# Moving a softmax's additions and a normalization's scaling from VectorE to GpSimd

## Chip, cores and metric

The kernel runs on one core of a Trainium2 chip. The metric is the device time of one execution in microseconds (us), as a median over runs. The engines of the core are TensorE (PE in the profile; its weight loads stand apart as PEld), VectorE (DVE), ScalarE (ACT), GpSimd (POOL) and SyncE (SP). Each has its own queue and takes its instructions in order; they wait for one another through semaphores.

## What is computed

A transformer block in float32 on x of 8 x 512 x 1024: softmax attention with 32 heads, a gated feed-forward layer, a causal sigmoid attention with 4 heads, and the same feed-forward layer again, each behind a layer norm and with its result added to x. The change touches the first part alone:

```python
def _layernorm(x, axis=-1, eps=1e-05):
    m = jnp.mean(x, axis=axis, keepdims=True)
    v = jnp.var(x, axis=axis, keepdims=True)
    return (x - m) / jnp.sqrt(v + eps)

def _L0_attn_a_ref(x, attn_qkvw, attn_qkvb, attn_ow, attn_ob):   # x is layer-normed
    HEADS = 32
    B, S, H = x.shape
    hd = H // HEADS
    scale = 1.0 / np.sqrt(hd)
    qkv = x @ attn_qkvw + attn_qkvb
    ...
    scores = jnp.einsum('bhqd,bhkd->bhqk', q, k) * scale
    probs = jax.nn.softmax(scores, axis=-1)
    ctx = jnp.einsum('bhqk,bhkd->bhqd', probs, v)
    ctx = jnp.transpose(ctx, (0, 2, 1, 3)).reshape(B, S, H)
    return ctx @ attn_ow + attn_ob

x = x + _L0_attn_a_ref(_layernorm(x, axis=-1), ...)
x = x + _L0_ffn_ref(_layernorm(x, axis=-1), ...)
x = x + _L0_attn_b_ref(_layernorm(x, axis=-1), ...)
x = x + _L0_ffn_ref(_layernorm(x, axis=-1), ...)
```

## The kernel before

The attention is cut into 64 units. Unit n is batch n // 8 and a group g = n % 8 of four heads, which together fill the 128 partitions. The loop over n (from line 1039) writes out by hand the order in which every engine gets its instructions: there is no scheduler, and what is written first is queued first.

A unit has four steps i of 128 keys or queries each. In step i the loop asks for

- `rows_step(n + 1, i)`: scores of the next unit with 128 queries on the partitions (L905, into the PSUM tile `sc`), and on DVE the row maxima with their sign turned (L906, `nmax`), which read `sc`;
- `between()`: a share of the side tasks and of the filler. The side tasks are small steps on DVE and DMA issues, kept in the queue `side` and spread over the five calls of a unit by `places`. The filler is PE work of other units: projections of unit n + 2 (L578, seven Strassen products gathered by L156 and L158), output projections (L788), and tiles of the next stage;
- `keys_step(n, i)`: the maxima are spread over `sc` by a matmul with ones (L934), the scores with keys on the partitions are added (L937), and ACT takes the exp of 128 x 2048 elements into a tile `pT` (L939). `pT` has three buffers, `sc` has one, which `rows_step` and `keys_step` share;
- `sum_step`: the four `pT` tiles of a unit are added up, as the softmax's denominators need it, into one tile `sum`. The first addition, of tiles 0 and 1, is made by GpSimd in two halves of 128 x 1024 (L948) behind the second exp. The other two are made by DVE, each one instruction of 128 x 2048 (L950): tile 2 is added ahead of step 3's `keys_step`, tile 3 in the first step of the next unit, behind its first `rows_step`.

`values_step` multiplies the exp tiles with v (L961) in step 2 and in step 0 of the next unit. `normalize(n - 1)` then sums `sum` over the partitions with a matmul (`den`, L973) and divides. At the end of a unit `split_max(n + 1)` cuts the finished maxima of the next unit into three bfloat16 parts, with five short DVE instructions: casts of `nmax` or `rest` into `parts` (L912, L914, L916) and subtractions of what the cast kept (L913, L915). Then, in step 0 of the next unit, `turn_max` turns the parts with PE (`tpm`, printed under L578) and ACT copies them into `shift` (L926), which L934 reads.

While the groups of batch b run, `norm_tasks(b + 1)` prepares the next batch. The turned x (`xT`, loaded as such) gets its layer norm there: statistics of the rows (L241, L242), the root by GpSimd (L249), one row of factors and one of shifts sent to DRAM and spread over all partitions (L550, L554), and then `apply` on `xT`: four pairs of a multiplication and an addition of 128 x 1024 elements (L558), by DVE. Eight lists of such tasks are handed out: lists 0 and 1 in unit g = 0, 2 and 3 in g = 1, 4 in g = 2, and the last three, with `apply` in them, in g = 3, 4 and 5. In g = 6 `left_tasks` forms the sums of `xT` that the projections multiply.

GpSimd's queue also holds DMA issues: weight sums (L613, L753) in the first nine units, rows of x after the attention (L816) and turned tiles (L876) later, and the roots of the layer norms (L249).

Of the kernel before, what the change touches and what calls it, by code (L numbers as in the profile page):

```python
# [17 lines left out]
ALU = mybir.AluOpType  # L18
# [8 lines left out]
TPB = S // P  # L27
# [3 lines left out]
GH = P // HD_A  # L31
# [42 lines left out]
class Filler:  # L74
# [47 lines left out]
    def run(self, count):  # L122

        while self.queue and count:
            count -= self._run_one() > 0
# [295 lines left out]
def softmax_attention(tc, cst, stage, filler, clusters, pools, dr, late, args):  # L421
# [11 lines left out]
    nc, small, ps_m = tc.nc, stage.small, stage.ps_m  # L433
# [16 lines left out]
    units, half = B * NC, NC // 2  # L450
# [25 lines left out]

    once = [partial(ow_source, RIGHT[k], c) for k in UPPER for c in range(half)]
    ows = Stream(nc, owpool, OW_BUFS, [P, S], "ow", once * (2 * B - 1))
    used, side, tiles, waiting, ready, held = {"w": 0}, deque(), deque(), deque(), deque(), []

    def first_norm():

# [37 lines left out]
    def norm_tasks(b):  # L520

        xT, st = xTp.tile([P, NC, S], F32, tag="xT", name=f"xT_{b}"), {}
        xTs[b] = xT

        def idle():
            pass

        def load(i):  # L530
            st[i] = xpool.tile([P, H], F32, tag="x", name=f"x_{b}_{i}")
            nc.sync.dma_start(st[i], x[ts(b * TPB + i, P), :])

        def turned(k):
            nc.sync.dma_start(xT[:, ts(k, 2), :], xT_in[b, :, ts(k, 2), :])

        def stats(i):
            if i == 0:
                st["mv"] = small.tile([P, TPB, 2], F32, tag="ln_mv", name="ln_mvs")
            stage.stats(st.pop(i), st["mv"][:, i, :])  # L540

        def root():
            st["rows"] = small.tile([P, 2, TPB], F32, tag="ln_rows", name="ln_rows")
            stage.rstd(st["mv"], TPB, st["rows"][:, 0, :])

        def shift():
            stage.shifts(st["mv"], st["rows"][:, 0, :], st["rows"][:, 1, :])

        def send():
            nc.sync.dma_start(dr.rows[b].rearrange("(k t p) -> p k t", k=2, p=P), st["rows"])  # L550

        def spread():
            st["all"] = xpool.tile([P, 2, S], F32, tag="x", name=f"rows_{b}")
            nc.sync.dma_start(st["all"].rearrange("p k s -> p (k s)"), dr.rows[b].partition_broadcast(P))  # L554

        def apply(k, j):
            part, rows = xT[:, ts(j, 2), :], st["all"][:, k, :].unsqueeze(1).to_broadcast([P, 2, S])
            nc.vector.tensor_tensor(part, part, rows, (ALU.mult, ALU.add)[k])  # L558

        scaled = [partial(apply, k, j) for j in range(NC // 2) for k in range(2)]  # L560
        return [
            [partial(load, 0), partial(load, 1)],
            [partial(turned, k) for k in range(NC // 2)] + [partial(stats, 0), partial(stats, 1)],
            [partial(load, 2), partial(load, 3)],
            [idle] * 3 + [partial(stats, 2), partial(stats, 3)],
            [root, shift, send, idle, spread],
            [idle, idle, *scaled[:3]],
            [idle, idle, *scaled[3:6]],
            [idle, idle, *scaled[6:]],
        ]  # L570

    width = [P]
# [98 lines left out]
    def left_tasks(b):  # L671

        xT = xTs[b]
        a11, a12, a21, a22 = (xT[:, ts(k, half), ts(m, 2 * P)] for m in range(2) for k in range(2))
        sums = (sump.tile([P, half, 2 * P], F32, tag=f"s{k}", name=f"s{k}_{b}") for k in (1, 2, 4))
        lefts[b], steps = left_sums(nc, a11, a12, a21, a22, *sums)
        return [lambda: run(enumerate(steps[:2])), *steps[2:]]
# [240 lines left out]
    def turn_max(n):  # L918

        st = state[n]  # L920
        tp = ps_m.tile([P, TPB, P], F32, tag="mm", name="tpm")
        for qt in range(TPB):
            part = parts[n % 2][:, qt, :, :].rearrange("p h c -> p (h c)")
            product(tp[:, qt, :], part, cst.ident_h, start=True, stop=True)
        st["shift"] = shiftp.tile([P, S], BF16, tag="shift", name=f"shift_{n}")
        nc.scalar.copy(st["shift"], tp.rearrange("p t q -> p (t q)"))  # L926
# [15 lines left out]
    def sum_step(n, kt):  # L942

        st = state[n]
        if kt == 1:
            st["sum"] = tmp.tile([P, GH, S], F32, tag="sum", name="sum")
            for h in (slice(0, GH // 2), slice(GH // 2, GH)):
                nc.gpsimd.tensor_tensor(st["sum"][:, h, :], st["pT", 0][:, h, :], st["pT", 1][:, h, :], ALU.add)  # L948
        else:
            nc.vector.tensor_tensor(st["sum"], st["sum"], st["pT", kt], ALU.add)  # L950

    def values_step(n, k):

# [30 lines left out]
    places, ow_later, last_sums, carried = [0], [], [], []  # L984

    def between(sides=True, form=2 * HD_A):


        if sides:
            for _ in range(-(-len(side) // places[0])):  # L990
                side.popleft()()
            places[0] -= 1
        width[0] = form
        filler.take()

    def mix_tile(near, wait):
        norm, logits = tiles.popleft()(blocks=wait)
        filler.mix(norm[:2], 0 if near else 2, 2 if near else 5)
        filler.mix(norm[2:], 9 if near else 14, 3)
        if wait:  # L1000
            waiting.append(logits)
        elif near:
            filler.mix(logits[:1], 16, 4)
            carried.extend(logits[1:])
        else:
            filler.mix(logits, 22, 4)

    def weave(pieces, products):

        out, at = [], 0  # L1010
        for j, product in enumerate(products):
            upto = 2 * round(len(pieces) * (j + 1) / (len(products) + 1) / 2)
            out += pieces[at:upto] + product
            at = upto
        return out + pieces[at:]
# [23 lines left out]
    for n in range(units):  # L1039
        b, g = divmod(n, NC)  # L1040
        ahead = n + 2
        if n == NC - 2:
            weights.fill(W_BUFS)
        if n == NC:
            run(next(outs))
            ows.fill(OW_BUFS)
        count = 0
        if n > NC:
            count = OUT_SHARES[(n - 1) % half] if n <= units - NC else LAST_SHARES[n - units]
        products = [next(outs) for _ in range(count)]  # L1050
        if ahead < units:
            if g == NC - 2:
                side.extendleft(reversed(left_tasks(b + 1)))
            filler.add(weave(project_pieces(ahead), products), mark=ahead)
        else:
            filler.add(weave([], products))
        ready.extend(waiting)
        waiting.clear()
        if tiles:
            mix_tile(n == units - 1, ahead < units)  # L1060
        side.extend(ow_later)
        ow_later.clear()
        if n == NC - 1:
            side.extend(last_sums)
        for c in OUT_SUMS.get(n, ()):
            load, steps = ow_sum_tasks(c)
            side.append(load)
            (ow_later if c == 0 else side).extend(steps)
        if b + 1 < B:
            if g == 0:  # L1070
                norms = deque(norm_tasks(b + 1))
            if g < 2:
                run(enumerate(norms.popleft()))
            if norms:
                side.extend(norms.popleft())
        side.extend(held)
        held.clear()
        filler.plan(FILLER_SHARES)
        places[0] = TPB + 1
        for i in range(TPB):  # L1080
            if n + 1 < units:
                rows_step(n + 1, i)
            if i == 0 and n > 0:
                sum_step(n - 1, TPB - 1)
            between()
            if i == 0:
                turn_max(n)
                between()
            if i == TPB - 1:
                sum_step(n, i - 1)  # L1090
            keys_step(n, i)
            if i == 1:
                sum_step(n, i)
            if i == 0 and n > 0:
                values_step(n - 1, 1)
                if ready:
                    by_cluster, by_token = ready.popleft()
                    run([by_cluster])
                    filler.mix([by_token], 6, 1)
                normalize(n - 1)  # L1100
            if i == 2:
                values_step(n, 0)
            between(False, HD_A if i in (0, 2) and n > 0 else 2 * HD_A)
        if n + 1 < units:
            split_max(n + 1)
        if ahead < units:
            filler.until(ahead)
    width[0] = P
    sum_step(units - 1, TPB - 1)
    ready = [make() for make in tiles]  # L1110
    tiles.clear()
    run(ready[0][0][:1])
# [8 lines left out]
    for i, (start, end) in enumerate(((0, 4), (4, 8), (8, 10), (10, 14))):  # L1121
        if i:
            ready = [make() for make in tiles]
# [601 lines left out]
```

## Time and profile before

| | |
|---|---|
| time, median of 3 runs | 3715.23 us (3713.79 to 3715.59) |
| span of the profiled execution | 3715.1 us |
| mean granted TensorE clock | 0.999 |
| PE busy, 356 to 2244 us (units 8 to 55) | 1886.08 of 1887.73 us |
| DVE busy, same stretch | 1336.87 us |
| ACT busy, same stretch | 502.98 us |
| GpSimd busy, same stretch | 264.00 us |

The profiled execution's span and the median of the runs are 0.1 us apart, so times of single rows can be set against the time of a run. The stretch of units 8 to 55 is periodic: a batch of eight units takes some 315 us. In it the sum of DVE's work is 71% of the time, GpSimd's 14%. A group of instructions in the profile is told by its line, engine, operation and tiles, as "L950 DVE TENSOR_TENSOR sum<-sum,pT"; behind the count stand busy time, the mean of one in ns, and the engine's idle time ahead of it, with what ended it.

### The profile page before, as it was taken

How to read it: one execution, taken by the hardware profiler on the slowest of the kernel's cores; microseconds unless marked ns; L12 is line 12 of the kernel's file. 1: busy time of each engine (PE TensorE's matmuls, PEld its weight loads, DVE VectorE, ACT ScalarE, POOL GpSimd, SP SyncE). 2: the span in 40 equal slices, each digit the busy share in tenths (PEclk: the TensorE clock that was granted, in tenths of full speed). 3: DMA queues.
4: the chain of work that ended last, by engine and by line, in shares of the span. 5: the costliest groups of instructions: out<-in, count | busy, mean ns of one | idle time of the engine just before them, and what ended most of it. 6: DMA issues, size and time to landing. Idle time of an engine off the chain costs nothing.

```text
span 3715.1 us, 76365 instructions
## 1 busy us (share of the span) xinstructions
PE 3677.4 (99%) x32792; PEld 1876.7 (51%) x32792; DVE 2539.7 (68%) x3497; ACT 927.8 (25%) x1017; POOL 594.9 (16%) x574
## 2 busy tenths in 40 slices
PE   8999999999999999999999999999999999999999
PEld 4444544544545455445445445444444467774444
DVE  4777676767667677766767767666788845556656
ACT  1222222222222222222222222222111144430000
POOL 1222111111111111111111111111000044530000
PEclk9999999999999999999999999999999999999999
DMA  5335444645655555465465454347566767763332
GB/s 184 113 122 179 142 143 147 192 138 157 185 153 150 159 162 163 133 198 152 139 182 159 143 150 124 122 156 244 158 180 179 184 186 234 222 220 127 133 132 98
DMA packets 728641, 598.55 MB, mean 161 GB/s; under 512 B 322152, under 2 KB 574064, under 8 KB 728304
## 3 DMA queue, kind: packets, MB, share of 16 engines
q1 hardware_dynamic: 701072, 496.40, 46.6%
q0 software_dynamic: 22912, 81.54, 5.7%
q10 hardware_dynamic: 4320, 15.73, 1.0%
q8 instruction: 259, 4.24, 0.5%
q14 instruction: 78, 0.64, 0.0%
HBM read 459.30 MB, written 134.25 MB: 160 GB/s over the span
## 4 chain that ended last, share of the span: by engine, by line
PE 95%; DVE 3%; DMA 1%; issue 1%; ACT 0%; POOL 0%; SPq 0%; DVEq 0%; ACTq 0%; POOLq 0%
PE mm L578 42%; PE dense L1285 20%; PE sc L905 7%; PE av L961 6%; PE sc L937 6%; PE csc L1347 4%; PE o L1366 4%; PE sc L934 2%; PE logitsT L339 1%; PE den L973 1%; PE tp L291 1%; DVE nmax L906 1%; DVE sum L950 1%; PE tpm L578 0%; DVE s L1377 0%
## 5 line engine op out<-in xcount | busy, mean ns | idle before, releaser
L906 DVE TENSOR_REDUCE nmax<-sc 128x4 f32<-128x2048 f32 x256 | 586.0, 2289 | 295.3 <-PE sc L905 295.2
L939 ACT ACTIVATE pT<-sc 128x2048 f32<-128x2048 f32 x256 | 480.8, 1878 | 1122.3 <-PE sc L937 1122.3
L948 POOL TENSOR_TENSOR sum<-pT,pT 128x1024 f32<-128x1024 f32 x128 | 309.4, 2438 | 750.0 <-ACT pT L939 678.1
L578 PE MATMUL mm<-xT,w 128*64 128x256 f32 (+1 forms) x3736 | 428.1, 383 | 0.0
L578 PEld LDWEIGHTS mm<-xT,w 128*64 128x64 f32 (+1 forms) x3736 | 241.5, 135 | 204.1 <-issue 54.3
L578 PE MATMUL mm<-s,w 128*32 128x256 f32 (+1 forms) x3672 | 321.2, 381 | 1.2 <-DVE qk L158 1.2
L950 DVE TENSOR_TENSOR sum<-sum,pT 128x2048 f32<-128x2048 f32 x128 | 292.0, 2281 | 0.9 <-ACT pT L939 0.9
L905 PE MATMUL sc<-qk,qk 32*64 32x512 f32 x4096 | 285.1, 613 | 0.5 <-ACT pT L939 0.4
L156 DVE TENSOR_TENSOR u<-dense,u 128x512 f32<-128x512 f32 x223 | 148.0, 685 | 184.7 <-PE dense L1285 169.3
L578 PEld LDWEIGHTS mm<-s,w 128*32 128x32 f32 (+1 forms) x3672 | 180.4, 122 | 180.4 <-issue 68.9
L937 PE MATMUL sc<-qk,qk 32*128 32x512 f32 x2048 | 263.7, 589 | 0.0
L578 PE MATMUL mm<-ow,ctxT 128*32 128x512 f32 (+2 forms) x1276 | 247.2, 599 | 3.0 <-DMA ow<-o_T 2.8
L961 PE MATMUL av<-pT,v 128*32 128x512 f32 x2048 | 246.4, 598 | 0.2 <-ACT pT L939 0.2
L1285 PE MATMUL dense<-sum,s 128*128 128x512 f32 x512 | 231.8, 593 | 0.0
L578 PEld LDWEIGHTS mm<-w,xT 128*64 128x64 f32 (+1 forms) x3888 | 197.5, 133 | 62.2 <-issue 48.9
L578 PE MATMUL mm<-w,xT 128*64 128x128 f32 (+1 forms) x3888 | 218.1, 274 | 0.0
L158 DVE SCALAR_TENSOR_TENSOR qk<-mm,qkvb_s,qk 128x256 f32<-128x256 f32 x224 | 107.6, 480 | 123.2 <-PE mm L578 119.2
L1285 PE MATMUL dense<-wT_s,dT_b 128*128 128x512 f32 x384 | 171.2, 593 | 0.0
L1285 PE MATMUL dense<-wT_s,dT_a 128*128 128x512 f32 x384 | 171.2, 593 | 0.0
L578 PE MATMUL mm<-ow,c 128*64 128x512 f32 (+2 forms) x864 | 169.9, 596 | 0.2 <-DMA ow<-in_ow 0.2
L578 PE MATMUL mm<-w,s 128*64 128x128 f32 x2688 | 162.5, 274 | 0.0
L578 PEld LDWEIGHTS mm<-w,s 128*64 128x64 f32 x2688 | 148.0, 137 | 22.9 <-issue 22.9
(236 smaller groups left out, 4468.8 us busy)
## 6 DMA issues: line engine op xcount, KB each, us to landing
w<-in_qkvw SPq DMA_DIRECT2D x252, 256.0 KB, 3.0
ow<-o_T SPq DMA_DIRECT2D x240, 256.0 KB, 3.6
w<-qk_T SPq DMA_DIRECT2D x224, 256.0 KB, 2.8
ow<-in_ow SPq DMA_DIRECT2D x180, 256.0 KB, 3.3
w<-v_T SPq DMA_DIRECT2D x112, 256.0 KB, 2.7
x<-in_x SPq DMA_DIRECT2D x32, 512.0 KB, 5.3
dT_a<-xT SPq DMA_DIRECT2D x32, 512.0 KB, 5.7
x_a<-x SPq DMA_DIRECT2D x32, 512.0 KB, 6.5
```

The source lines that it names most:

```text
L156: nc.vector.tensor_tensor(out, acc, other, ALU.add)
L578: nc.tensor.matmul(out[cols], lhsT[:, cols], rhs, **flags)
L905: nc.tensor.matmul(sc[ts(j, P // 2), h, :], st["q"][rows, cols], st["k"][rows, :], start=True, stop=True)
L906: nc.vector.tensor_reduce(st["nmax"][:, qt, :], sc, AX.X, ALU.max, negate=True)
L937: nc.tensor.matmul(sc[:, h, :], st["k"][rows, ts(kt, P)], st["q"][rows, :], start=False, stop=True)
L939: nc.scalar.activation(pT, sc, AF.Exp, scale=SCALE_A)
L948: nc.gpsimd.tensor_tensor(st["sum"][:, h, :], st["pT", 0][:, h, :], st["pT", 1][:, h, :], ALU.add)
L950: nc.vector.tensor_tensor(st["sum"], st["sum"], st["pT", kt], ALU.add)
L961: nc.tensor.matmul(st["av"][rows, :], st["v"][:, kt, rows], pT[:, h, :], start=(kt == 0), stop=(kt == TPB - 1))
L1285: nc.tensor.matmul(st["acc"], st["left"][LEFT[k]][:, c, :], self.w[RIGHT[k]][:, c, :], start=(c == 0), stop=(c == half - 1),)
L1347: nc.tensor.matmul(sc[:, AT_OFF[i] : AT_OFF[i] + n], k[:, c, ts(i, P)], xT[:, c, i * P :], start=(c == 0), stop=(c == 1),)
L1366: nc.tensor.matmul(acc[:, j - jj, :], at[:, start : start + P], self.v[b * TPB + i][:, cols], start=(i == 0), stop=(i == j),)
```

## The change

All three additions of a unit are made by GpSimd, each in two halves of 128 x 1024, and each is queued directly behind the `keys_step` that made its second operand: tiles 0 and 1 in step 1 as before, tile 2 in step 2, tile 3 in step 3. `apply` runs on GpSimd too. Its tasks no longer go into `side` but into a queue of their own, `slow`, which `between` empties in its second and third call of a unit, around `turn_max` and in step 1. The three lists lose the `idle` places that they began with, and `side` is shorter by them.

```diff
-    used, side, tiles, waiting, ready, held = {"w": 0}, deque(), deque(), deque(), deque(), []
+    used, side, slow, tiles, waiting, ready, held = {"w": 0}, deque(), deque(), deque(), deque(), deque(), []
...
             part, rows = xT[:, ts(j, 2), :], st["all"][:, k, :].unsqueeze(1).to_broadcast([P, 2, S])
-            nc.vector.tensor_tensor(part, part, rows, (ALU.mult, ALU.add)[k])
+            nc.gpsimd.tensor_tensor(part, part, rows, (ALU.mult, ALU.add)[k])
...
-            [idle, idle, *scaled[:3]],
-            [idle, idle, *scaled[3:6]],
-            [idle, idle, *scaled[6:]],
+            scaled[:3],
+            scaled[3:6],
+            scaled[6:],
...
             st["sum"] = tmp.tile([P, GH, S], F32, tag="sum", name="sum")
-            for h in (slice(0, GH // 2), slice(GH // 2, GH)):
-                nc.gpsimd.tensor_tensor(st["sum"][:, h, :], st["pT", 0][:, h, :], st["pT", 1][:, h, :], ALU.add)
-        else:
-            nc.vector.tensor_tensor(st["sum"], st["sum"], st["pT", kt], ALU.add)
+        before = st["pT", 0] if kt == 1 else st["sum"]
+        for h in (slice(0, GH // 2), slice(GH // 2, GH)):
+            nc.gpsimd.tensor_tensor(st["sum"][:, h, :], before[:, h, :], st["pT", kt][:, h, :], ALU.add)
...
             places[0] -= 1
+            if TPB - 2 <= places[0] < TPB and slow:
+                for _ in range(-(-len(slow) // (places[0] - TPB + 3))):
+                    slow.popleft()()
...
-                side.extend(norms.popleft())
+                (slow if len(norms) < 4 else side).extend(norms.popleft())
...
-            if i == 0 and n > 0:
-                sum_step(n - 1, TPB - 1)
             between()
             if i == 0:
                 turn_max(n)
                 between()
-            if i == TPB - 1:
-                sum_step(n, i - 1)
             keys_step(n, i)
-            if i == 1:
+            if i:
                 sum_step(n, i)
...
     width[0] = P
-    sum_step(units - 1, TPB - 1)
```

## Prediction

> **What bounds the kernel now.** I read the page's busy times first, then its chain of waits, then the groups of the lines that the diff touches.
>
> ```profile
> PE 3677.4 (99%) x32792; PEld 1876.7 (51%) x32792; DVE 2539.7 (68%) x3497; ACT 927.8 (25%) x1017; POOL 594.9 (16%) x574
> PE 95%; DVE 3%; DMA 1%; issue 1%; ACT 0%; POOL 0%; SPq 0%; DVEq 0%; ACTq 0%; POOLq 0%
> L948 POOL TENSOR_TENSOR sum<-pT,pT 128x1024 f32<-128x1024 f32 x128 | 309.4, 2438 | 750.0 <-ACT pT L939 678.1 <-ACT lg_a L350 40.3 <-DVE c L785 31.6
> L950 DVE TENSOR_TENSOR sum<-sum,pT 128x2048 f32<-128x2048 f32 x128 | 292.0, 2281 | 0.9 <-ACT pT L939 0.9
> L558 DVE TENSOR_TENSOR xT<-xT,rows 128x1024 f32<-128x1024 f32 x56 | 73.1, 1308 | 0.2
> ```
>
> TensorE (PE) is busy 99% of the span, and 95% of the chain is PE. From 356 to 2502 us, nearly all of the 64 attention units, PE's waits name VectorE (DVE) for 1.4 + 1.2 + 1.0 = 3.6 us in all. So relief for DVE is worth at most that, and the question is whether a new wait reaches PE. For that I read the timeline at the end of a unit (unit 39; columns: start and duration in us, engine, line, operation, tiles).
>
> ```profile
> 1602.42 1.88 ACT L939 ACTIVATE pT<-sc 128x2048 f32<-128x2048 f32 x1 [8.43 <-PE sc L937]
> ...
> 1605.42 0.19 DVE L912 CAST parts<-nmax 128x16 bf16<-128x16 f32 x1
> 1605.65 0.18 DVE L913 TENSOR_TENSOR rest<-nmax,parts 128x16 f32<-128x16 f32 x1
> ...
> 1605.87 0.20 DVE L914 CAST parts<-rest 128x16 bf16<-128x16 f32 x1
> ...
> 1606.11 0.19 DVE L915 TENSOR_TENSOR rest<-rest,parts 128x16 f32<-128x16 f32 x1
> 1606.33 0.20 DVE L916 CAST parts<-rest 128x16 bf16<-128x16 f32 x1
> 1606.41 2.28 DVE L906 TENSOR_REDUCE nmax<-sc 128x4 f32<-128x2048 f32 x1
> ...
> 1607.79 0.39 PE L578 MATMUL tpm<-ident_h,parts 128*64 128x128 bf16 x8
> ...
> 1609.84 0.40 PE L934 MATMUL sc<-shift,ones_h 32*128 32x512 bf16 x4
> ...
> 1612.76 1.04 PE L973 MATMUL den<-sum,ones 128*32 128x512 f32 x8
> ```
>
> Call t the end of a unit's fourth exp, here 1602.42 + 1.88 = 1604.30. The split of the next unit's maxima (L912 to L916) runs on DVE from t+1.12 to t+2.23; PE turns its result (tpm) at t+3.49, uses the scores' PSUM again (L934) at t+5.54 once nmax L906 has left it, and needs the finished sum (den) at t+8.46.
>
> Last, two places of the timeline where a GpSimd addition met DVE work; the single line at 157 us runs beside the second half of an addition pair that GpSimd ends at 158.71.
>
> ```profile
> 2361.97 0.68 DVE L785 TENSOR_TENSOR c<-ctxT 128x512 f32<-128x512 f32 x1
> ...
> 2362.65 5.25 POOL L948 TENSOR_TENSOR sum<-pT,pT 128x1024 f32<-128x1024 f32 x2 [31.59 <-DVE c L785]
> 2362.69 2.93 DVE L785 TENSOR_TENSOR c<-c,ctxT 128x512 f32<-128x512 f32 x1
> ...
> 2365.54 2.28 DVE L906 TENSOR_REDUCE nmax<-sc 128x4 f32<-128x2048 f32 x1
> ...
> 2367.87 0.40 PE L934 MATMUL sc<-shift,ones_h 32*128 32x512 bf16 x4 [0.86 <-DVE nmax L906]
> ```
>
> ```profile
> 157.87 0.87 DVE L248 TENSOR_SCALAR ln_rows<-ln_mvs 128x4 f32<-128x4 f32 x1
> ```
>
> A DVE addition of two SBUF operands, 0.69 us elsewhere, took 2.93: it was issued just after a GpSimd half-addition (2.41 us each) had begun and ended at 2365.62, 0.56 us after that one's end at 2365.06. GpSimd's second half then ended at 2367.90, 2.28 us after DVE. They take turns, an instruction at a time. L248, with one SBUF operand, took 0.87 instead of 0.16 and ended 0.03 us after the half-addition beside it. PE felt the first case: 0.86 us idle at L934. L906, which reads PSUM, is never slowed (2.28 to 2.29).
>
> **The change, part by part.**
>
> *Two DVE additions a unit go.* 128 x 2.28 = 292 us of DVE; worth 0 to 3.6 us on PE. I take 0.
>
> *Four half-additions a unit come on GpSimd*, 2.41 and 2.37 us a pair. After the fourth exp they end at t+0.15+4.78 = t+4.93, and den comes at t+7.2 to t+9.5 in units 0 to 61 and at t+6.6 in unit 62: hidden, and without that cover each would cost up to 4.9. An exp tile has three buffers, so up to unit 62 the next write of one comes over 15 us after its addition can start. In unit 63 there is no cover: its exps end at 2511.18, 2514.84 and 2520.35, so the additions run 2511.3 to 2516.1 and 2516.1 to 2520.9, two DMA issues of 0.57 follow, and the last runs 2522.1 to 2526.9; den stood at 2522.82. **+4.1.**
>
> *Where the additions lie.* The split follows gathers that wait for PE, so it stays where it is from unit 6 on, and the new pair of half-additions runs from t+0.15 to t+2.56 and on: over it. L913 and L915 read two SBUF operands. L912, L914 and L916 read one, and the trace shows no such cast beside GpSimd. Bounds: freely, as L248 of one element a partition does (11 times beside a GpSimd multiply, 0.15 us), or turn by turn, as L248 of four elements did. A cast from SBUF runs at the two-fold rate (L1434, 1024 elements, 0.674 us; L415 from PSUM, 512 elements, 0.692), so I take it to use what the additions use, and let it wait.
>
> *The price of a unit.* A released instruction ends 0.05 to 0.06 us after GpSimd's (its 0.19 or 0.20 less the 0.13 that 0.69 - 0.56 shows); GpSimd's next takes 2.28. So the locked ones leave at t+2.62, 4.95, 7.28, 9.61, 11.94, as long as GpSimd has something queued. Without a scaling behind it, GpSimd is empty after the second: L912 leaves at 2.62, L913 at 4.95, L916 at 5.65 (0.70 further, as in the rows), tpm starts at 5.71. Late by 5.71 - 3.49 = 2.22. Late next is nmax: 5.53 to 7.82, L934 at 7.87 instead of 5.54 + 2.22: 0.11 more. 2.33 in units 0, 4, 5, 7 of a batch; where tpm and L934 stood at 3.55 and 5.71 (unit 1) 2.16; at 4.36 and 6.41 (unit 6) 1.46.
>
> *The scaling* (56 operations of 1216 ns on DVE, alone; 2.3 to 2.4 on GpSimd) is put behind that pair: the order of GpSimd's queue in the changed kernel has three of them directly behind the last addition of a batch's unit 2, two behind that of unit 3, one behind that of unit 4, before anything that waits. Its rows have landed by then (issued at t-7.5, 7.8 to land). They keep the turns going: unit 2, L916 leaves at 11.94, tpm 12.00 against 4.36, and 0.11: 7.75. Unit 3: L915 at 9.61, tpm 9.89 against 3.70: 6.19. Unit 4: L914 at 7.28, tpm 7.80 against 3.49, and 0.11: 4.42.
>
> A batch: 3 x 2.33 + 2.16 + 7.75 + 6.19 + 4.42 + 1.46 = 28.97; six batches (units 8 to 55) **+173.8**. Units 6, 7 and 56 to 62, by the same t+5.71 against their tpm (t+2.62, 2.88, 2.63, 2.88, three of the first kind, one of 1.46, t+2.51): 3.09 + 2.83 + 3.08 + 2.83 + 6.99 + 1.46 + 3.20 = **+23.5**. In units 0 to 5 the split waits only for the DVE addition that goes, so it moves ahead of t: 0.
>
> *Queues.* PE's, ACT's and SP's orders are unchanged. GpSimd's DMA issues (x1, turned x, weight sums) fall up to 5 us later behind additions; what reads them comes a stage or at least a unit later: 0.
>
> Sum: 173.8 + 23.5 + 4.1 = 201.4. On the profiled execution's 3715.1 us: **3916**; the runs' median, 3715.23, is the same within 0.2 us.
>
> [...]
>
> **The rivals.**
>
> *The casts pass freely* (for it: L248 of one element; against: the two-fold rate). L913 leaves at 2.61, GpSimd's second half ends at 4.89, L915 leaves at 4.94, L916 at 5.16, tpm 5.22: 1.84 in units 0, 4, 5, 7; 1.67, 0.97, 1.52, 0.97 in 1, 2, 3, 6; the scaling costs nothing. 6 x 12.49 + 23.5 - 9 x 0.49 + 4.1 = 98.1: 3813.
>
> [...]
>
> *Not slower*: 16 elements slip past GpSimd's reads as the one-element L248 does. It decides if L913 beside a half-addition stays under 1.2 us, the room between L916 and tpm in most units. Then at most 3.6 and the 1.4 of den's wait are won and 4.1 lost: 3714 to 3719, 3717. Against it: 4 elements (L248) and 64 (L394, 1.30 instead of 0.23) waited.
>
> *More than the turns*: DVE's lateness reaches gathers or weights too, over 3960.
>
> **How the numbers follow.** Forecast 0.60, casts free 0.19, one turn 0.06, not slower 0.07, more 0.08. The forecast's own range: down to 3841 if the scalings come too late to take turns (units 2 to 4 then cost 1.46, 2.01 and 2.33: 6 x 12.56 less), up to 3927 if GpSimd's turns take 2.41. The range takes in the casts-free case: 3800 to 3960. A change under 0.2% (7.4 us) can't be told from none: faster 0.02, same 0.05, slower 0.93.
>
> **What would show it.** Right: L912 and L913 about 1.4 and 2.2 us long, PE's waits for tpm on DVE L916 near 190 us, L906 unchanged, DVE's busy time not lower by 365 us. The casts decide between forecast and first rival: L914 and L916 of 2 us in units 2 to 4 of a batch, or 0.2. Wrong if split instructions stay at 0.2 us beside GpSimd, or if PE waits at den or the exps on GpSimd.

## The result and the profile after

The changed kernel takes 3967.05 us (median of four runs, 3965.66 to 3967.57) against 3714.82 us: a ratio of 1.0677, with a 95% interval of 1.0662 to 1.0692. That is 252 us more, where the forecast was 201 and the range ended at 3960. The page of the kernel after, its busy times and its chain of waits:

```profile
PE 3750.1 (95%) x32792; PEld 1895.9 (48%) x32792; DVE 2461.9 (62%) x3313; ACT 933.9 (24%) x1017; POOL 1323.7 (33%) x886
PE 87%; DVE 10%; DMA 1%; issue 1%; POOL 0%; SPq 0%; ACT 0%; DVEq 0%; POOLq 0%; ACTq 0%
```

DVE now holds 10% of the chain, and DVE's busy time fell by 78 us only, though 365 us of instructions left it. And PE, whose instructions are the same 32,792 in the same order, is busy 72.7 us longer (3750.1 against 3677.4). The view of PE's waits (what waited, for what; us in total, times, the longest) has two lines that the change touches, first as they were before, then after:

```profile
PE tpm L578 <- DVE parts L916: 1.3, 2, 1.0
PE den L973 <- DVE sum L950: 1.4, 1, 1.4
...
PE tpm L578 <- DVE parts L916: 180.3, 58, 7.4
PE den L972 <- POOL sum L949: 3.4, 2, 2.8
```

Where DVE's time went is told by the groups of the split's lines, which took 185 to 203 ns each before, beside the maxima L906, which kept their 2.29 us, and GpSimd's new work:

```profile
L906 DVE TENSOR_REDUCE nmax<-sc 128x4 f32<-128x2048 f32 x256 | 586.0, 2289 | 318.7 <-PE sc L905 318.7
L913 DVE TENSOR_TENSOR rest<-nmax,parts 128x16 f32<-128x16 f32 x64 | 130.2, 2035 | 2.2
L912 DVE CAST parts<-nmax 128x16 bf16<-128x16 f32 x64 | 71.5, 1116 | 0.1
L914 DVE CAST parts<-rest 128x16 bf16<-128x16 f32 x64 | 52.5, 820 | 2.2
L915 DVE TENSOR_TENSOR rest<-rest,parts 128x16 f32<-128x16 f32 x64 | 37.3, 582 | 2.2
L916 DVE CAST parts<-rest 128x16 bf16<-128x16 f32 x64 | 25.4, 398 | 2.2
L949 POOL TENSOR_TENSOR sum<-sum,pT 128x1024 f32<-128x1024 f32 x256 | 600.2, 2365 | 555.4 <-ACT pT L939 555.4
L558 POOL TENSOR_TENSOR xT<-xT,rows 128x1024 f32<-128x1024 f32 x56 | 130.9, 2348 | 0.7
```

The same unit 39 as before, from the timeline of the kernel after (start and duration in us); its fourth exp ends at t = 1749.24 + 1.88 = 1751.12:

```profile
1751.26 4.67 POOL L949 TENSOR_TENSOR sum<-sum,pT 128x1024 f32<-128x1024 f32 x2 [5.61 <-ACT pT L939]
1752.24 1.44 DVE L912 CAST parts<-nmax 128x16 bf16<-128x16 f32 x1
1753.71 2.26 DVE L913 TENSOR_TENSOR rest<-nmax,parts 128x16 f32<-128x16 f32 x1
...
1756.01 0.20 DVE L914 CAST parts<-rest 128x16 bf16<-128x16 f32 x1
1756.25 0.18 DVE L915 TENSOR_TENSOR rest<-rest,parts 128x16 f32<-128x16 f32 x1
1756.46 0.20 DVE L916 CAST parts<-rest 128x16 bf16<-128x16 f32 x1
...
1756.72 0.41 PE L578 MATMUL tpm<-ident_h,parts 128*64 128x128 bf16 x8 [1.95 <-DVE parts L916]
...
1756.97 1.90 PE L578 MATMUL mm<-xT,w 128*64 128x256 f32 x16
```

The split starts at t+1.12 as before. L912 leaves behind GpSimd's first half-addition, L913 behind its second, and the split ends at t+5.54 instead of t+2.23; tpm starts at t+5.60. Unit 26 is a batch's unit 2 (t = 1173.79), with three scalings queued behind the pair:

```profile
1178.56 7.06 POOL L558 TENSOR_TENSOR xT<-xT,rows 128x1024 f32<-128x1024 f32 x3
...
1178.68 2.28 DVE L914 CAST parts<-rest 128x16 bf16<-128x16 f32 x1
1181.00 2.37 DVE L915 TENSOR_TENSOR rest<-rest,parts 128x16 f32<-128x16 f32 x1
1183.40 2.28 DVE L916 CAST parts<-rest 128x16 bf16<-128x16 f32 x1
...
1185.73 0.64 PE L578 MATMUL tpm<-ident_h,parts 128*64 128x128 bf16 x8 [7.42 <-DVE parts L916]
...
1186.16 3.62 PE L578 MATMUL mm<-xT,w 128*64 128x256 f32 x16
```

All three late instructions, two casts among them, take a turn of 2.3 us each, and PE waits 7.42 us. The last row holds what the forecast lacks: 16 products that took 1.90 us in unit 39 take 3.62 here. The view by stretches (length, PE's busy time and instructions, the granted clock, DMA share, GB/s) shows the wait, the 4.3 us behind it, and what follows:

```profile
1178.40:1185.70 7.30, 0.00 (x0) 0.83 0.12 36
1185.70:1190.00 4.30, 4.27 (x28) 0.50 0.00 0
1190.00:1194.00 4.00, 4.00 (x44) 1.00 0.26 66
```

Behind the wait PE runs at half its clock until 1190.0, with no DMA traffic beside it. The clock's records change in steps of 3.413 us. Over the execution they hold 183 us at one half; before, 10.

As PE's instructions are the same in the same order, the time from each start to the next can be set against before, one by one. Worked out so from the two traces: 187.3 us more ahead of the first tpm of a unit (57 of the 64 come late), 64.0 us more behind instructions that started at half clock (838 of them, 83.0 us before and 147.0 after), and -1.2 us in the other 31,896. The sum is 250.1 us; the spans differ by 250.3. PE's busy time grew by 72.7 us and not by 64.0, since some 8 of the 187.3 us are counted as busy: ahead of a wait of 1.95 us tpm is 2.12 us late, and the other 0.17 are counted with the product before it.

### The profile page after: what moved, and what is told of

Same layout as the page of the kernel before. It is cut to its first block, busy times and chain, and to the rows that moved or that the text cites. A ratio compares the mean times of both kernels' runs of the same rounds, so it can differ in the third digit from the quotient of the medians.

```text
span 3965.4 us, 76573 instructions
## 1 busy us (share of the span) xinstructions
PE 3750.1 (95%) x32792; PEld 1895.9 (48%) x32792; DVE 2461.9 (62%) x3313; ACT 933.9 (24%) x1017; POOL 1323.7 (33%) x886
## 4 chain that ended last, share of the span: by engine, by line
PE 87%; DVE 10%; DMA 1%; issue 1%; POOL 0%; SPq 0%; ACT 0%; DVEq 0%; POOLq 0%; ACTq 0%
PE mm L578 38%; PE dense L1282 19%; PE av L960 6%; PE sc L937 6%; PE sc L905 5%; PE o L1363 3%; PE csc L1344 3%; DVE rest L913 3%; PE sc L934 2%; DVE parts L912 2%; PE logitsT L339 1%; PE den L972 1%; DVE parts L914 1%; DVE rest L915 1%; PE tpm L578 1%
## 5 line engine op out<-in xcount | busy, mean ns | idle before, releaser
L949 POOL TENSOR_TENSOR sum<-sum,pT 128x1024 f32<-128x1024 f32 x256 | 600.2, 2365 | 555.4 <-ACT pT L939 555.4
L906 DVE TENSOR_REDUCE nmax<-sc 128x4 f32<-128x2048 f32 x256 | 586.0, 2289 | 318.7 <-PE sc L905 318.7
L578 PE MATMUL mm<-xT,w 128*64 128x256 f32 (+1 forms) x3736 | 469.2, 409 | 0.0
L578 PEld LDWEIGHTS mm<-xT,w 128*64 128x64 f32 (+1 forms) x3736 | 256.5, 144 | 220.8 <-issue 105.0
L937 PE MATMUL sc<-qk,qk 32*128 32x512 f32 x2048 | 272.2, 607 | 0.0
L578 PE MATMUL tpm<-ident_h,parts 128*64 128x128 bf16 x512 | 30.7, 251 | 180.3 <-DVE parts L916 180.3
L156 DVE TENSOR_TENSOR v<-mm,v 128x256 f32<-128x256 f32 x196 | 80.2, 421 | 175.7 <-PE mm L578 174.9
L975 DVE STREAM_TRANSPOSE rden<-den 128x512 f32<-128x512 f32 x64 | 45.9, 717 | 211.7 <-PE den L972 211.7
```

What stands on the lines that cost most here:

```text
L156: nc.vector.tensor_tensor(out, acc, other, ALU.add)
L578: nc.tensor.matmul(out[cols], lhsT[:, cols], rhs, **flags)
L906: nc.vector.tensor_reduce(st["nmax"][:, qt, :], sc, AX.X, ALU.max, negate=True)
L937: nc.tensor.matmul(sc[:, h, :], st["k"][rows, ts(kt, P)], st["q"][rows, :], start=False, stop=True)
L949: nc.gpsimd.tensor_tensor(st["sum"][:, h, :], before[:, h, :], st["pT", kt][:, h, :], ALU.add)
```

## The experiments

Two explanations of PE's longer work were set against each other: the clock, halved where PE has stood idle, and GpSimd's traffic in SBUF, as GpSimd is busy more than twice as long (1323.7 us against 594.9). All kernels were timed beside the kernel before on the same chip (3714.9 us for the first four, 3715.2 for the others).

**The additions alone** (edit against the changed kernel; the three lists and the queue go back with it):

```diff
-            nc.gpsimd.tensor_tensor(part, part, rows, (ALU.mult, ALU.add)[k])
+            nc.vector.tensor_tensor(part, part, rows, (ALU.mult, ALU.add)[k])
...
-                (slow if len(norms) < 4 else side).extend(norms.popleft())
+                side.extend(norms.popleft())
```

> All three additions on GpSimd as in the change, the scaling back on DVE. Two theories for the 64 to 73 us by which PE's own work grew in the changed kernel. Clock: PE's granted clock is halved for a stretch of 3.41 us or more after PE has stood idle through most of one, so only waits of 4 to 7 us (units 2 to 4 of a batch) cost much of it. Traffic: GpSimd's reads and writes of SBUF slow PE's own work in proportion. Without the scaling the turns end with the second half-addition in every unit, so both expect waits for tpm near 100 us, none over 2.4 us. Clock then expects PE's busy time up by 5 to 25 us on 3677 and about 3835 us (3815 to 3855). Traffic expects 600 of 728 us of GpSimd's added work to remain, so PE's busy time up by some 60 us, and about 3880 us.

Measured: 3867.6 us, ratio 1.0415 (1.0400 to 1.0431), and PE's waits for tpm

```profile
PE tpm L578 <- DVE parts L916: 105.9, 58, 4.0
```

The waits came as forecast, 1.95 us in most units, but for five in units 6, 7, 56, 57 and 62 of 2.5 to 4.0 us, where none over 2.4 was expected; the time lies between the two expectations. In the profiled execution, the slowest of the four (3874.8 us; the fastest took 3863.4), PE's busy time is up by 53.7 us, which looks like the traffic. Matched instruction by instruction it isn't: 112.8 us ahead of those 57 tpm, 43.4 at half clock (502 instructions), 1.7 in the other 32,232. What was wrong is the belief that a 2 us wait doesn't halve the clock. In this run it did, in some units and not in others, by where it fell. Three stretches of this kernel in a row, cut where the clock's records begin and end, and three around another such wait:

```profile
1056.50:1059.90 3.40, 1.45 (x20) 1.00 0.97 357
1059.90:1063.30 3.40, 3.40 (x20) 0.50 0.07 20
1063.30:1066.70 3.40, 3.40 (x52) 1.00 0.29 82
...
1268.10:1271.50 3.40, 2.94 (x34) 1.00 0.34 106
1271.50:1274.90 3.40, 1.92 (x24) 1.00 0.29 82
1274.90:1278.30 3.40, 3.38 (x42) 1.00 0.27 77
```

The wait of unit 24 (1.95 us) lies whole in one stretch, PE is busy 1.45 of 3.40 us, and the next stretch runs at half clock. That of unit 29, as long, is cut by a border (0.46 and 1.48 us idle), and the clock stays whole.

**The scaling alone** (against the kernel before: `apply` on GpSimd and handed out by `slow`, the additions as they were):

> Only the scaling on GpSimd, queued where the change queues it; the second and third addition on DVE at their old places. The scaling of a batch's unit 2 starts when its rows have landed, 0.3 us after the fourth exp, and lies over the split; that of units 3 and 4 starts in the middle of a unit. By turns instruction by instruction L912 leaves at about 2.65, L913 at 5.0 and L914 at 7.4 us after the exp, tpm 3.7 us late in unit 2 of each of six batches: 22 us of waits for tpm, and by the clock theory up to 13 us more behind them: 3737 to 3752. By the traffic theory the growth of PE's work is 13 us wherever it falls. If the scaling were free on GpSimd (only the additions matter): 3715.

Measured: 3736.6 us, ratio 1.0061 (1.0046 to 1.0076), 0.4 us under the expected range. PE waits 18.1 us for tpm, 2.7 to 3.1 us in unit 2 of each of the six batches and, as before, 1.0 us near the end; its work is 7.2 us longer at half clock. The scaling costs little by itself; behind a third addition it is what makes waits of 4 to 7 us out of those of 2.

**The third addition behind the split:**

```diff
+    seen = tmp.tile([P, 1], BF16, name="seen")
...
-            if i:
+            if i in (1, 2):
                 sum_step(n, i)
...
             split_max(n + 1)
+            nc.gpsimd.tensor_copy(seen, parts[(n + 1) % 2][:, TPB - 1, GH - 1, 2:3])
+        sum_step(n, TPB - 1)
```

> As the change, but the third addition stands behind the split: GpSimd first copies one element of the split's last result, then adds; the scaling stands behind that as before. Turns theory: the overlap with the split is gone, the additions run from 2.3 to 7.1 us after the exp and den needs them at 8.5; waits for tpm under 5 us, clock 0.99 or more, PE's busy time as before, 3715 to 3722 with the 4 us at the last unit. Traffic theory: the same GpSimd work as in the change, so PE's busy time stays 50 to 70 us higher: about 3780. If the cause of the waits were not the overlap but GpSimd being late with what others need: waits for den in their place, over 3800.

Measured: 3724.6 us, ratio 1.0028 (1.0017 to 1.0039). The waits for tpm are gone but for the one of 1.0 us that the kernel before has, and PE's busy time is 3677.7 us, as before, although GpSimd does all that it does in the changed kernel (1341.5 us). So the traffic theory falls, and the overlap with the split is the cause of the waits. The time is 2 to 3 us above the expected range. One cause is in the timeline, in unit 3 of each batch (lines here are one further on; L907 is the maxima, L935 the use of `sc`):

```profile
1140.70 2.36 POOL L559 TENSOR_TENSOR xT<-xT,rows 128x1024 f32<-128x1024 f32 x1
1140.76 2.31 DVE L261 SCALAR_TENSOR_TENSOR ln_shift<-ln_mv,ln_rstd 128x1 f32<-128x1 f32 x1
1142.99 2.28 DVE L907 TENSOR_REDUCE nmax<-sc 128x4 f32<-128x2048 f32 x1
...
1145.33 0.40 PE L935 MATMUL sc<-shift,ones_h 32*128 32x512 bf16 x4 [1.02 <-DVE nmax L907]
```

A DVE instruction of one element a partition but with two inputs in SBUF, 0.15 us elsewhere, waits out a scaling, the maxima behind it are late, and PE waits 1.02 us: six times. (The one-element L248, 0.15 us each time in the kernel before, has one input.)

**The same work in smaller pieces** (the additions as below, the scaling in the same manner, four pieces for one):

```diff
-        for h in (slice(0, GH // 2), slice(GH // 2, GH)):
-            nc.gpsimd.tensor_tensor(st["sum"][:, h, :], before[:, h, :], st["pT", kt][:, h, :], ALU.add)
+        for h in range(GH):
+            for c in range(2):
+                at = ts(c, S // 2)
+                nc.gpsimd.tensor_tensor(st["sum"][:, h, at], before[:, h, at], st["pT", kt][:, h, at], ALU.add)
```

> As the change, in the same places, but each addition cut into eight of 128x256 and each scaling operation into four of 128x256. Turns an instruction at a time: a turn is 0.6 to 0.7 us instead of 2.3, the split's five instructions leave in five turns and L916 ends near 4.0 us after the exp instead of 5.6, and the scaling behind it costs nothing: PE waits 0.4 to 0.6 us a unit, some 30 us in all, no halving of the clock, about 3750 us (3735 to 3770), although GpSimd's busy time is higher than in the change. If DVE had to wait until GpSimd's queue is empty: as the change, 3967. Traffic theory: waits gone but PE's work still 60 us longer, about 3810.

Measured: 3780.7 us, ratio 1.0178 (1.0163 to 1.0193), 11 us above the expected range. The additions are where they are in the changed kernel and GpSimd is busy 194 us longer, yet 186 of the 252 us are gone. The last three of the split's instructions in the timeline of one unit (lines are three further on):

```profile
1718.84 0.67 DVE L917 CAST parts<-rest 128x16 bf16<-128x16 f32 x1
1719.55 0.63 DVE L918 TENSOR_TENSOR rest<-rest,parts 128x16 f32<-128x16 f32 x1
1720.21 0.67 DVE L919 CAST parts<-rest 128x16 bf16<-128x16 f32 x1
...
1720.93 0.41 PE L581 MATMUL tpm<-ident_h,parts 128*64 128x128 bf16 x8 [0.75 <-DVE parts L919]
```

A turn is 0.7 us, the length of a piece, for casts as for subtractions. PE waits 0.75 us in most units, 47.2 us in all; expected were 0.4 to 0.6 and 30, as a turn was taken some 0.07 us too short, five times a unit. At half clock, of which none was expected, PE's work is 9.1 us longer, not 64. With five pieces in a row on GpSimd, DVE took three turns of 0.63 to 0.67 us beside them: it takes its turn behind each instruction, not behind GpSimd's queue.

**PE kept busy while it waits** (against the changed kernel, in `turn_max`):

```diff
+        if NC <= n < units - 1:
+            for _ in range({1: 6, 2: 6, 3: 30, 4: 25, 5: 16, 6: 6, 7: 2, 0: 6}[n % NC] if NC < n <= units - NC else 6):
+                nc.tensor.matmul(tp[:, 0, :], cst.ident, cst.ident, start=True, stop=True)
```

> As the change in every engine's work, but PE gets extra products ahead of the turning of the split's parts: 6 to 30 fp32 products of 128x128 (estimated 0.22 us each from the 0.45 us of a 128x512 row) into a PSUM tile that the turning then overwrites, sized to end shortly before the split does: some 140 us of added PE work in all. Clock theory: PE no longer stands idle for most of a 3.41 us stretch, the clock stays near 1.0, and 60 of the 64 us by which PE's other work was longer are gone: about 3905 us (3890 to 3925), faster than the change although PE does more. Traffic theory: GpSimd's work is the same, so 3967 or more.

Measured: 3913.2 us, ratio 1.0534 (1.0518 to 1.0550) to before: 54 us faster than the changed kernel, with 624 products more. In place of the 7.42 us wait of unit 26 stands PE's added work, and the 16 products behind it take 1.90 us, not 3.62:

```profile
1157.95 6.96 PE L924 MATMUL tpm<-ident 128*128 128x128 f32 x60
...
1165.49 0.41 PE L578 MATMUL tpm<-ident_h,parts 128*64 128x128 bf16 x8 [0.58 <-DVE parts L916]
1165.74 1.90 PE L578 MATMUL mm<-xT,w 128*64 128x256 f32 x16
```

The mean clock is 0.996 (0.977 in the changed kernel). GpSimd's work is the same to 0.2 us. This is the term that the forecast lacks, taken out by itself.

**Waits of chosen length, without GpSimd** (against the kernel before, ahead of the split):

```diff
+        if NC < n <= units - NC:
+            for _ in range((10, 12, 14, 17, 21, 28)[(n - 1) // NC - 1]):
+                nc.vector.tensor_tensor(rest, st["nmax"], part[:, :, :, 0], ALU.subtract)
```

> The kernel before with GpSimd's work untouched; only DVE repeats the split's first subtraction 10, 12, 14, 17, 21 and 28 times ahead of the split, one count for each of the six batches of units 8 to 55, so that PE waits for tpm some 1.0, 1.5, 2.0, 2.5, 3.5 and 5.0 us a unit. Clock theory: no stretch of halved clock in the first two batches, three to five in the third, about five in the fourth, seven or eight in the fifth, ten or more in the sixth, each costing PE about 1.5 us, in all some 42 us besides 138 us of waits: about 3895 us (3875 to 3920). Traffic theory: PE's busy time as before and about 3853 us. If a wait of 2.0 us never halves the clock, the changed kernel's 2 us waits were not what cost it.

Measured: 3894.0 us, ratio 1.0482 (1.0467 to 1.0496), a microsecond from the expectation. By batches, matched with the kernel before as above (us; the wait is that of most units):

```
wait of a unit   tpm later   at half clock   PE's work longer there   rest
0.8              10.7        0.0             0.0                      1.8
1.3              14.2        3.4             1.6                      1.8
1.7              18.0        6.9             2.9                      1.7
2.35             23.5        20.4            9.3                      1.4
3.2              31.1        22.0            8.1                      0.3
4.8              36.9        46.3            16.5                     -0.2
```

In the profile's own view by stretches, the second and the last of these batches:

```profile
710.00:1042.00 332.00, 318.14 (x3702) 0.99 0.53 152
...
2085.00:2453.00 368.00, 331.91 (x3700) 0.94 0.44 125
```

The work is the same in both, and PE is busy 13.8 us longer in the last. In units 1 and 3 of a batch, where the split had no slack, waits are some 1.2 us longer than the table says. The one halving of the second batch, where none was expected, and both of the third stand behind such waits, of 2.5 to 3.1 us; waits of 1.7 us and less halved nothing.

**The changed kernel's delays, without GpSimd** (the same edit with 11 to 39 repetitions by the unit of the batch):

> The kernel before with GpSimd's work untouched; DVE repeats the split's first subtraction 11 to 39 times ahead of the split, so that the split ends as late as in the changed kernel, unit by unit of a batch (15 times in most). Clock theory: waits for tpm near 180 us and PE's busy time up by 55 to 80 us as in the change: 3935 to 3975. Traffic theory: the waits alone, about 3895 us.

Measured: 3975.6 us, ratio 1.0701 (1.0686 to 1.0715). This is 0.6 us over the expected range. Waits for tpm are 190.7 us; PE's work is 53.1 us longer at half clock, 6.0 us elsewhere. With no more GpSimd work than before, a late split alone makes the changed kernel's time, and 9 us more, as its waits are 10 us longer in all.

**The additions behind the split, the scaling and the last two units' third addition on DVE** (against the run with the third addition behind the split; the scaling goes back to DVE as in the run with the additions alone):

```diff
+        if kt == TPB - 1 and n > units - 3:
+            nc.vector.tensor_tensor(st["sum"], st["sum"], st["pT", kt], ALU.add)
+            return
```

> The third addition behind the split as in the run before, all scaling back on DVE, and the third addition of the last two units on DVE: what is left of the change is 126 units' additions taken from DVE, 280 us of its work. If DVE's relief is worth nothing on PE: 3713 to 3717, not to be told from the kernel before. If the relief shortens a wait that the profile doesn't show: under 3711. If the 10 us that the run before cost came from the additions and not from the scaling and the last unit: 3720 or more.

Measured: 3712.2 us (median of eleven runs) against 3715.2: ratio 0.9991 (0.9982 to 1.0000), which can't be told from no change: a gain, if there is one, is under 0.2%. DVE is busy 2306.2 us instead of 2539.7, and that buys nothing that can be measured. It is no better kernel than the one before, only the change without its cost.

## Why the prediction was right and wrong

**The turns of DVE and GpSimd: right.** The split ends at t+5.54 in unit 39 (forecast t+5.65), and tpm starts at t+11.94 in unit 26 (12.00) and at t+9.74 and t+7.69 in units 27 and 28 (9.89, 7.80). The casts wait as the subtractions do: no row of before showed one beside GpSimd, so that was my estimate, and unit 26 shows L914 and L916 at 2.28 us beside L915 at 2.37. L906 is untouched (at most 2.29 us, before and after), and in the smaller pieces a turn is 0.7 us, the length of one GpSimd instruction there. So the casts-free rival and "not slower" fall, and so does the "one turn" of the chances, by which the five leave together: L912 and L913 left in two turns in unit 39, the last three in three more in unit 26.

**The scaling keeps the turns going: right**, in units 2, 3 and 4 of a batch, with 7.4, 6.1 and 4.0 us of wait. By itself it costs 22 us; with the additions it makes 100 (3967 against 3868), as it lengthens both the waits and the halved stretches behind them.

**DVE's relief is worth nothing: right.** The last run shows it: 3712.2 us against 3715.2 with 234 us less work on DVE.

**The last unit: right.** Forecast 4.1, measured 4.4: den ended 7.93 us after the last exp (2774.14 - 2766.21) instead of 3.53 (2523.88 - 2520.35).

**The step that failed** is the sum, "A batch: 3 x 2.33 + 2.16 + 7.75 + 6.19 + 4.42 + 1.46 = 28.97". It prices each unit by how late tpm comes and takes PE's own work behind the wait at the durations of before. The lateness came near: 187.3 us against 173.8 + 23.5 = 197.3. Of the difference some 4 us are the 0.11 us that the forecast adds for nmax in most units, which this count has behind tpm, and the others turns a little shorter than forecast (tpm 2.12 us late in most units, not 2.22). But PE's work behind the waits ran at half clock, 3.4 or 6.8 us a time by the clock's records (once 10.2), and took 64.0 us longer in all. A batch took 351.6 us instead of 315.5: tpm 27.5 later, 8.6 from the clock. With it the forecast's terms come to 201.4 + 64.0 = 265 us, where 252 were measured. The rival "more than the turns" had the size, over 3960, but not the mechanism: of all that the change touches, PE's waits name the split's result for 180.3 us and the sum for 3.4.

The profile of before could have told it. Behind the attention it has a wait of 2.57 us, for a transfer, and the stretches around it read:

```profile
2567.20:2570.60 3.40, 0.83 (x3) 1.00 1.02 393
2570.60:2574.00 3.40, 3.40 (x4) 0.50 1.10 357
2574.00:2577.40 3.40, 3.40 (x14) 1.00 0.92 232
```

There is another in the attention, ahead of the 356 us from which the prediction read PE's waits: at 293.64 us PE had waited 2.30 us for nmax on DVE, the next stretch ran at half clock, and the eight products of L937 in it took 1.90 us instead of 1.03. I read the clock only as its mean, 0.999, and that is a fact about a kernel in which PE hardly ever waits. The clock's records of both kernels hold no value but 1.0 and 0.5, in steps of 3.413 us, and as the run with the additions alone shows, a wait of 1.95 us sufficed for a half (unit 24).

## What to carry to other kernels

A wait that is put on a saturated PE can cost more than its length: in the changed kernel, 187.3 us of late tpm brought 64.0 us of longer work behind them. Price the wait, then ask whether most of a stretch of 3.413 us becomes idle (the share from which the clock halved is in the next section), and add what the work behind it loses at half clock (0.37 us for each us of halved stretch in the changed kernel, 0.32 to 0.46 in the runs with the additions alone and with DVE's delays). Beside GpSimd's additions and scalings of 2.3 to 2.4 us, the split's subtractions and casts took up to 2.37 us on DVE instead of 0.2; where such work lies on PE's path, put GpSimd's behind it by a dependence (3724.6 us here instead of 3967), or cut it small (3780.7). And work taken from an engine that the bound doesn't wait for bought nothing here, though 234 us left DVE in the last run.

## What was not expected of the hardware

The halving was a matter of phase in these runs. I took PE's idle share from the matmuls' records on the grid of the clock's records, for stretches that ran at full clock behind the start of the program. In before, after and all runs without added products, every stretch with an idle share over 0.59 was followed by half clock, none of 0.56 or less was, and in between most were (31 of 39). (In the run with added products two more were, at 0.52 and 0.55.) A wait of 1.95 us is 0.57 of a stretch, so it halved the clock only where it lay in one stretch whole: with the additions alone, three to five times a batch of eight units, and never in the first of the six batches. Even so it didn't always: three such waits of that run, 0.57 of a stretch, left the clock whole.

In the changed kernel the batches fall into step with that grid: from the second on each takes 351.6 us, 103 stretches, with the same four halvings. The run with DVE's delays settles at 355.0 us, 104 stretches. Why was not tried.
